# Moving four loads of a graph attention kernel to other places in the DMA queue

## Chip, cores and metric

The kernel runs on one core of a Trainium2 chip. The metric is the device time of one execution in microseconds, the median of several runs; lower is better. TensorE (PE in the profile) multiplies matrices and reads its weights with separate load instructions (PEld); VectorE is DVE, ScalarE is ACT, GpSimd is POOL. SyncE (SP) does no arithmetic here: its sequencer (SPq) issues the DMAs of the main loop one after the other, and a DMA that has to wait for a semaphore holds up everything behind it in that queue.

## What is computed

For each of 16 batch entries there are 512 nodes with 512 features, and each node attends to the first 20 nodes. Cut to what matters here:

```python
row_zero = v.sum(-1) == 0                                  # flags: which rows of x are zero
q_exp = where(row_zero, 0, q)
self_feat = concat([v, q_exp]) @ W_self.T + b_self
output = self_feat
for d in range(2):                                         # adj and its transpose
    A = adj (d == 0) or swapaxes(adj, 1, 2) (d == 1), first 20 columns     # 11 int32 labels each
    cond, vb = A.sum(-1), A @ w_bias + b_bias              # mask, and a bias from the labels
    aff = (self_feat @ Wq.T + bq) . (kv @ Wk.T + bk) / sqrt(dh)            # 16 heads, dh = 32
    w = softmax(where(cond > 0, aff, NEG) + vb)
    output += heads(w @ kv) @ Wout + bout
return v + relu(output)
```

## The kernel before

**Set-up** (lines 453 to 760) folds the key projections into the queries' weights and writes to DRAM what each batch entry needs later: the keys `g_d`, the values `bd_d` (fetched as `vd`), the score biases `cq_d`.

**The main loop** (lines 781 to 963) runs over the entries b, and in each over four tiles nt of 128 nodes. Everything is in float32. The order on each engine is written out by hand. Entry b+1 is prepared while entry b is worked on. TensorE's order within one entry, from the output product on, is:

- nt = 2: `attend(b-1)` (line 426, 48 small matmuls into the four banks `ps_o`: the weighted values of the entry before, called the output product here), the scores of tile 2 (line 353, 128 matmuls into `ps_s`), products 1 and 2 of entry b+1 (line 279). The self features are computed with seven half-size products in place of eight, numbered 1 to 7; 1, 4, 6 and 7 go to `ps_a`, 2 to `ps_d`, 3 and 5 to `ps_c`.
- nt = 3: product 6, the scores of tile 3, products 7 and 5.
- then entry b+1 begins. nt = 0: product 4, the scores of tile 0 in two parts (feature blocks 0 and 1 of the keys, then 2 and 3), and product 3, which is the last of the seven.
- nt = 1: the scores of tile 1.

VectorE takes the scores from `ps_s` (`weigh`, lines 367 to 375), ScalarE exponentiates (380), VectorE sums and inverts (406, 407), GpSimd scales (408), VectorE transposes (415). VectorE also adds the flag term to the products (`partial`, line 286, which needs the flags `nz`). GpSimd adds masks and biases of a tile (`full_add`, line 341, which needs `cq`) and x to the output (`residual`, line 444). ScalarE multiplies the labels of a half (two tiles) by the weights (`mask_mul`, line 314, which needs `adj`) and spreads the result over heads (334).

**SP's queue in one entry b** (for 0 < b < 15), with what each DMA waits for:

- nt = 0: x of b+1 in two halves (line 105), the first behind the exp of the tile before, the second behind `partial(b, 4)`; the flags of b+1 to DRAM (171, behind `row_mask` on GpSimd); the first half of the masks, `adj(b+1, 0)` (114), behind `mask_sum` of b.
- nt = 1: the flags read back to all partitions, `nz` (175), behind the exp of tile 0; the score biases `cq`, four DMAs (119); the second half of the masks, `adj(b+1, 1)`, behind `normal` on GpSimd.
- nt = 2: the rows of x of b+2 for the flags, `xn`, in two halves (109), the first behind the first of the four additions of `finish` (435), the second behind its first relu (439); the first half of the keys (130) behind the exp of tile 2.
- nt = 3: the output of b-1, blocks 0 and 1 (449, each behind its `residual`); the second half of the keys behind `mask_sum(b+1, 0)`; output block 2; the values `vd` (136); output block 3 follows at the next nt = 0.

`adj` has three buffers, `nz`, `cq` and `xn` have two. A manual dependency is added by `behind(dma, instruction)` (line 95).

Of the kernel before, what the change touches and what calls it, by code (L numbers as in the profile page):

```python
# [18 lines left out]
def gat_kernel(  # L19
# [81 lines left out]
    def load_x(b, ks=range(C), ins=None):  # L101
        if ks[0] == 0:
            xs[b] = load.tile([P, C, N], F32, tag="x", name=f"x{b}", bufs=3)
        at = slice(ks[0], ks[-1] + 1)
        behind(nc.sync.dma_start(xs[b][:, at], xT[b].rearrange("(c p) n -> p c n", p=P)[:, at]), ins)
# [5 lines left out]
    def load_adj(b, h, ins=None):  # L111
        t = adjs[b, h] = load.tile([P, 2, S * L], I32, tag="adj", name=f"adj{b}_{h}", bufs=3)
        a = adj[b, h * 2 * P : (h + 1) * 2 * P].rearrange("(t p) d m l -> p t (d m l)", p=P)
        behind(nc.sync.dma_start(t, a), ins)
# [317 lines left out]
    def finish(b, o, banks):  # L432

        for c in range(C):
            add = nc.vector.tensor_add(o[:, c], banks[c], sfs[b][:, c])  # L435
            if c == 0:
                done["add"] = add
        for c in range(C):
            relu = nc.scalar.activation(o[:, c], o[:, c], AF.Relu, bias=bo[:, c : c + 1])  # L439
            if c == 0:  # L440
                done["relu"] = relu

    def residual(b, c, o):
        nc.gpsimd.tensor_add(o[:, c], o[:, c], xs[b][:, c])  # L444
        outs.append((b, c, o))
# [323 lines left out]
    with tc.manual_schedule():  # L769
# [11 lines left out]
        for b in range(B):  # L781
            more = b + 1 < B
# [6 lines left out]
            for nt in range(NT):  # L789
# [22 lines left out]
                if nt == 0:  # L812
                    if b == 0:
                        for g in range(2):
                            scores(b, nt, g, ps[g])
                        mask_sum(b, 1)
                    else:
                        mask_mul(b, 1)
                        product(b, 4)
                        for g in range(2):  # L820
                            scores(b, nt, g, ps[g], range(2))
                        normal(*prev)
                        partial(b, 4, 1, 0, block(b, 1, 0))
                        if more:
                            load_x(b + 1, range(2), done["exp"])
                            load_x(b + 1, range(2, C), done["partial"])
                        for g in range(2):
                            scores(b, nt, g, ps[g], range(2, C))
                        if more:
                            row_mask(b + 1)  # L830
                        mask_count(b, 1)
                        joined(b, 3, "c", 1, 1)
                        product(b, 3)
                        mask_sum(b, 1)
                        if more:
                            load_adj(b + 1, 0, done["masks"])
                    mask_spread(b, 1, (0, 1))
                    if last:
                        biased = work.tile([P, C, N], F32, tag="o", name="biased")
                        for c in (2, 3):  # L840
                            nc.scalar.activation(biased[:, c], sfs[b][:, c], AF.Identity, bias=bo[:, c : c + 1])
                    s = weigh(b, nt, pair)
                    expo(s)
                    mask_spread(b, 1, (2, 3))
                    if prev is not None:
                        turn(*prev)
                    full_add(b, 1)
                    if more:
                        x_sum(b + 1, 1)
                    else:  # L850
                        for c in (2, 3):
                            nc.gpsimd.tensor_add(biased[:, c, N - P :], biased[:, c, N - P :], xs[b][:, c, N - P :])

                if nt == 1:
                    if b > 0:
                        joined(b, 2, "c", 0, 1)
                    if b > 0 and more:
                        load_nz(b + 1, done["exp"])
                        load_cq(b + 1)
                    normal(*prev)  # L860
                    if b > 0 and more:
                        load_adj(b + 1, 1, done["normal"])
                    if b == 0:
                        self_feat(0, 1, 1)
                    for g in range(2):
                        scores(b, nt, g, ps[g])
                    if b == 0:
                        self_copy(0, 1, 1)
                    if last:
                        for c in (0, 1):  # L870
                            nc.scalar.activation(biased[:, c], sfs[b][:, c], AF.Identity, bias=bo[:, c : c + 1])
                    s = weigh(b, nt, pair)
                    expo(s)
                    turn(*prev)
                    if more:
                        x_sum(b + 1, 2)
                        x_sum(b + 1, 3)
                    full_add(b, 2)
                    if last:
                        for c in (0, 1):  # L880
                            nc.gpsimd.tensor_add(biased[:, c], biased[:, c], xs[b][:, c])  # L881

                if nt == 2:
                    if more:
                        mask_mul(b + 1, 0)
                    else:
                        full_add(b, NT - 1)
                    if b > 0:
                        banks = [bank(f"ps_o{b - 1}_{q}", q) for q in range(4)]
                        attend(b - 1, banks)  # L890
                        o = work.tile([P, C, N], F32, tag="o", name=f"o{b - 1}")
                        finish(b - 1, o, banks)
                        if b + 2 < B:
                            load_xn(b + 2, 0, done["add"])
                            load_xn(b + 2, 1, done["relu"])
                    normal(*prev)
                    for g in range(2):
                        scores(b, nt, g, ps[g])
                    if more:
                        product(b + 1, 1)  # L900
                        product(b + 1, 2)
                    s = weigh(b, nt, pair, (lambda: partial(b + 1, 1, 0, 0)) if more else None)
                    expo(s)
                    turn(*prev)
                    if b > 0 and more:
                        load_keys(b + 1, range(2), done["exp"])
                    if more:
                        full_add(b, NT - 1)
                    if b > 0:
                        for c in (0, 1):  # L910
                            residual(b - 1, c, o)

                if nt == 3 and more:
                    mask_count(b + 1, 0)
# [131 lines left out]
```

## Time and profile before

| | us |
|---|---|
| runs of the kernel before | 590.48, 591.52, 591.87 (median 591.52) |
| the profiled execution, its own time | 593.27 |
| span of its profile, first to last instruction | 591.5 |
| mean granted TensorE clock | 0.995 |

How to read the views: the page gives each engine's busy time and its share of the span. The chain that ended last lists, in order of time, the work that each step waited for: start, duration, engine, tile, line, count; "issue" is time in which the engine waited for nothing that the profile shows. The view of waits gives, for an engine and a line, who ended its idle time, the total, the count and the longest. The timeline lists instructions in order of time (start, duration, engine, line, operation, tiles, count). The view of windows gives for a stretch its length, then each engine's busy time and number of instructions, the clock, the mean busy share of the 16 DMA engines and the GB/s. The DMA view lists queues (packets, MB, share of the DMA engines) and issues (count, size of each, median time from issue to landing).

### The profile page before, as it was taken

Reading aid. Unit: us, or ns where it says so; the run is one execution under the profiler, and the core shown is the slowest. Engines: PE = TensorE matmul, PEld = TensorE weight load, DVE = VectorE, ACT = ScalarE, POOL = GpSimd, SP = SyncE. Lnnn points to the kernel's source line nnn. Section 1 sums busy time; section 2 is a strip of 40 time slices with the busy share of each in tenths; the row PEclk is TensorE's granted clock in tenths of the full one; section 3 lists DMA queues with packets and bytes.
Section 4 is the critical chain, followed back from the end, with each engine's and each line's share of the span. In section 5 each row is a group of like instructions: output and inputs, shape, how many; then the busy total and the mean of one; then the engine's idle time right before and its main releaser. Section 6 shows DMA issues by size and latency. Waiting matters only on the chain.

```text
span 591.5 us, 30038 instructions
## 1 busy us (share of the span) xinstructions
PE 578.7 (98%) x13180; PEld 439.7 (74%) x13180; DVE 492.3 (83%) x785; ACT 395.6 (67%) x1162; POOL 384.2 (65%) x351
## 2 busy tenths in 40 slices
PE   8999999999999999999999999999999999999994
PEld 6654547888978687787878787788787878787882
DVE  0495565889898888999999999888989898989896
ACT  1234644587877677768686868677787877777661
POOL 2315663638677675758686777675858677776774
PEclk9999999999999999999999999999999999999997
DMA  8998999857848485767676766757585748582503
GB/s 294 385 406 299 332 376 329 257 126 199 223 154 229 155 236 148 206 168 209 184 208 163 223 173 202 171 181 208 164 217 170 216 149 232 158 238 85 167 13 142
DMA packets 98129, 124.10 MB, mean 210 GB/s; under 512 B 19952, under 2 KB 70160, under 8 KB 95952
## 3 DMA queue, kind: packets, MB, share of 16 engines
q1 hardware_dynamic: 96752, 120.31, 67.1%
q8 instruction: 103, 1.69, 1.2%
q0 software_dynamic: 672, 1.36, 1.0%
q10 hardware_dynamic: 576, 0.53, 0.3%
q14 instruction: 26, 0.21, 0.1%
HBM read 82.30 MB, written 40.24 MB: 207 GB/s over the span
## 4 chain that ended last, share of the span: by engine, by line
PE 94%; DVE 3%; DMA 1%; issue 1%; ACT 0%; POOL 0%; SPq 0%; DVEq 0%; POOLq 0%; ACTq 0%
PE ps_s L353 44%; PE ps_a L279 17%; PE ps_c L279 8%; PE ps_o L426 6%; PE ps_d L279 4%; PE ps_v L644 3%; PE ps_k L581 3%; PE ps_sf L202 2%; DMA ws_q<-in_wsT 1%; PE ps_kv L532 1%; DVE o L435 0%; PE ps_nz L186 0%; DVE wt L415 0%; DVE ps_s L371 0%; DVE sm L406 0%
## 5 line engine op out<-in xcount | busy, mean ns | idle before, releaser
L353 PEld LDWEIGHTS ps_s<-g,sf 128*32 128x32 f32 x8192 | 264.0, 110 | 19.8 <-issue 12.2
L353 PE MATMUL ps_s<-g,sf 128*32 128x152 f32 x8192 | 277.3, 293 | 0.5 <-ACT st L684 0.5
L334 ACT COPY both<-add 32x80 f32<-32x80 f32 x512 | 130.9, 256 | 54.8 <-DVE add L325 49.0
L408 POOL TENSOR_TENSOR s<-s,sm 128x640 f32<-128x640 f32 x63 | 80.3, 1275 | 98.0 <-DVE sm L407 98.0
L341 POOL TENSOR_TENSOR full<-cq,both 128x640 f32<-128x640 f32 x64 | 100.1, 1565 | 30.3 <-issue 24.3
L314 ACT ACTIVATE prod<-adj,wb_sb 128x80 f32<-128x80 int32 x330 | 112.5, 432 | 0.0
L380 ACT ACTIVATE s<-s 128x640 f32<-128x640 f32 x63 | 46.5, 738 | 69.4 <-DVE s L375 69.0
L444 POOL TENSOR_TENSOR o<-o,x 128x512 f32<-128x512 f32 x60 | 75.9, 1285 | 0.0
L367 DVE TENSOR_TENSOR full<-ps_s,full 128x608 f32<-128x608 f32 x63 | 49.1, 779 | 32.1 <-PE ps_s L353 26.6
L406 DVE TENSOR_REDUCE sm<-s 128x32 f32<-128x640 f32 x63 | 50.9, 808 | 8.8 <-ACT s L380 8.6
L279 PE MATMUL ps_a<-t,ws_s 128*32 128x246 f32 x960 | 55.5, 370 | 0.0
L371 DVE TENSOR_REDUCE ps_s<-full 128x32 f32<-128x640 f32 x63 | 52.2, 828 | 2.2
L415 DVE STREAM_TRANSPOSE wt<-s 128x640 f32<-128x640 f32 x63 | 52.8, 839 | 0.1
L375 DVE TENSOR_TENSOR s<-full,ps_s 128x640 f32<-128x640 f32 x63 | 51.6, 818 | 1.1
L426 PE MATMUL ps_o<-wt,vd 32*32 32x512 f32 (+5 forms) x816 | 40.8, 581 | 3.7 <-DVE wt L400 2.0
L279 PEld LDWEIGHTS ps_a<-t,ws_s 128*32 128x32 f32 x960 | 32.2, 110 | 15.5
L325 DVE TENSOR_REDUCE add<-prod 128x80 f32<-128x960 f32 x32 | 36.8, 1150 | 6.3 <-ACT prod L314 4.4
L244 POOL TENSOR_TENSOR t<-x 128x492 f32<-128x492 f32 x30 | 34.4, 1148 | 10.1 <-DVE full L367 5.2
L439 ACT ACTIVATE o<-o,bo 128x512 f32<-128x512 f32 x60 | 38.2, 708 | 0.6 <-POOL biased L881 0.6
L435 DVE TENSOR_TENSOR o<-ps_o,sf 128x512 f32<-128x512 f32 x60 | 36.8, 672 | 1.0 <-PE ps_o L426 1.0
L286 DVE SCALAR_TENSOR_TENSOR u<-nz,qw,ps_a 128x246 f32<-128x246 f32 x90 | 36.6, 449 | 0.0
L244 POOL TENSOR_TENSOR t<-x,t 128x492 f32<-128x492 f32 x30 | 34.4, 1147 | 1.2
(238 smaller groups left out, 722.7 us busy)
## 6 DMA issues: line engine op xcount, KB each, us to landing
g_d<-st SPq DMA_DIRECT2D x16, 1064.0 KB, 5.9
g<-g_d SPq DMA_DIRECT2D x28, 608.0 KB, 5.2
out_T<-o SPq DMA_DIRECT2D x60, 256.0 KB, 4.7
xn<-in_xn SPq DMA_DIRECT2D x28, 512.0 KB, 3.6
x<-in_xT SPq DMA_DIRECT2D x28, 512.0 KB, 4.3
adj<-in_adj SPq DMA_DIRECT2D x32, 440.0 KB, 5.0
nz<-nz_d SPq DMA_DIRECT2D x14, 256.0 KB, 4.0
wk<-in_wkT SPq DMA_DIRECT2D x2, 1024.0 KB, 8.0
```

Source lines behind the costliest of these rows:

```text
L244: nc.gpsimd.tensor_sub(t, one, two)
L279: nc.tensor.matmul(to, lhs, x[:, k], start=start, stop=stop, skip_group_check=n != 2)
L314: nc.scalar.activation(p[:, :, l], a[:, :, l], AF.Identity, scale=wb_sb[:, l : l + 1])
L334: nc.scalar.copy(adds[b, h][bass.ts(a, R), :, g], add[r].rearrange("p (t m) -> p t m", t=2))
L341: nc.gpsimd.tensor_add(f, cqs[b].unsqueeze(1).to_broadcast(shape), adds[b, nt // 2][:, nt % 2].unsqueeze(2).to_broadcast(shape),)
L353: nc.tensor.matmul(bank[bass.ts(a, R), bass.ts(j, WD // HL)], sfs[b][:, k, bass.ds(nt * P + (2 * g + j) * R, R)], keys[:, k, a], start=(k ...
L371: nc.vector.tensor_reduce(mx, f, AX.X, ALU.max)
L375: nc.vector.tensor_sub(s, f, mx.unsqueeze(3).to_broadcast(full))
L408: done["normal"] = nc.gpsimd.tensor_mul(s, s, sm.unsqueeze(3).to_broadcast(full))
L415: nc.vector.transpose(wts[b][:, nt], s.rearrange("p a h m -> p (a h m)"))
L426: nc.tensor.matmul(banks[a][bass.ds(at // 2 * DH, n * DH)].rearrange("p (t n) -> p t n", n=32), vd[r, bass.ds(at * DH, n * DH)], wt[r, :, ...
L444: nc.gpsimd.tensor_add(o[:, c], o[:, c], xs[b][:, c])
```

## The change

In every entry b from 1 to 14:

- `adj(b+1, 0)` is issued directly behind the second half of x, ahead of the flags' write to DRAM, with no wait of its own (it waited for `mask_sum` before).
- `nz` is issued in nt = 2, after `finish` in program order, with the same kind of wait (the last exp, now that of tile 1).
- `done["add"]` becomes the last of the four additions in `finish`, so the first `xn` waits for the fourth addition in place of the first.
- after the residuals of blocks 0 and 1 in nt = 2 the output of these blocks is stored there (before: at the start of nt = 3, the next place in SP's queue), and behind the stores come `adj(b+1, 1)` and the four DMAs of `cq`, with no wait of their own.

Nothing else is touched: the same loads, of the same sizes, and the same arithmetic.

```diff
@@ finish
             add = nc.vector.tensor_add(o[:, c], banks[c], sfs[b][:, c])
-            if c == 0:
-                done["add"] = add
+            done["add"] = add
@@ nt == 0
                             load_x(b + 1, range(2), done["exp"])
                             load_x(b + 1, range(2, C), done["partial"])
+                            load_adj(b + 1, 0)
...
                         mask_sum(b, 1)
-                        if more:
-                            load_adj(b + 1, 0, done["masks"])
@@ nt == 1
                         joined(b, 2, "c", 0, 1)
-                    if b > 0 and more:
-                        load_nz(b + 1, done["exp"])
-                        load_cq(b + 1)
                     normal(*prev)
-                    if b > 0 and more:
-                        load_adj(b + 1, 1, done["normal"])
@@ nt == 2
                         finish(b - 1, o, banks)
+                        if more:
+                            load_nz(b + 1, done["exp"])
                         if b + 2 < B:
                             load_xn(b + 2, 0, done["add"])
...
                             residual(b - 1, c, o)
+                        store()
+                        if more:
+                            load_adj(b + 1, 1)
+                            load_cq(b + 1)
```

## The prediction

> **What bounds the kernel now.** First the page.
>
> ```profile
> span 591.5 us, 30038 instructions
> ...
> PE 578.7 (98%) x13180; PEld 439.7 (74%) x13180; DVE 492.3 (83%) x785; ACT 395.6 (67%) x1162; POOL 384.2 (65%) x351
> ```
>
> TensorE is busy for 98% of the span. The change removes no work, so it can only win back time in which TensorE stands still. The second view, the chain in order of time, shows where that is. These are output products (line 426, the start of nt = 2) from three stretches of it.
>
> ```profile
> 164.12 2.60 PE ps_o L426 x47
> ...
> 195.02 1.04 PE ps_o L426 x25
> 196.06 0.39 issue
> 196.45 2.10 PE ps_o L426 x23
> ...
> 226.92 0.98 PE ps_o L426 x4
> ...
> 258.97 2.17 PE ps_o L426 x48
> ...
> 289.44 2.17 PE ps_o L426 x48
> ...
> 381.08 1.05 PE ps_o L426 x27
> ...
> 413.08 2.84 PE ps_o L426 x48
> ...
> 444.22 2.17 PE ps_o L426 x48
> ...
> 535.83 2.17 PE ps_o L426 x48
> ```
>
> An undisturbed entry takes 289.44 - 258.97 = 30.47 us. Five entries take longer: from 164.12 to 195.02 it is 30.90, then 31.90, then 32.05 (to 258.97); from 381.08 32.00, then 31.14 (to 444.22). Over 30.48 that is 0.42 + 1.42 + 1.57 + 1.52 + 0.66 = **5.6 us**. The twelve entries from 164.12 to 535.83 take 371.71 against 12 x 30.48 = 365.76, so 5.95 us are lost in all, nearly all of it in these products. The loss is "issue": no semaphore ended it, and it begins behind 25, 4 or 27 matmuls, so no operand was missing at the start.
>
> What is left is the supply of instructions. The page's queue list has one for them, and the DMA view of two stretches (0 to 225.9, 0 to 288.55) and the windows say how far it had come.
>
> ```profile
> q8 instruction: 103, 1.69, 1.2%
> ...
> q8 instruction: 31, 0.51, 0.9%
> ...
> q8 instruction: 44, 0.72, 1.0%
> ```
>
> ```profile
> 0.00:225.90 225.90, 221.91 (x4117) 159.77 (x4121) 165.71 (x276) 130.37 (x373) 125.22 (x128) 1.00 0.82 264
> 0.00:288.55 288.55, 284.09 (x5688) 208.45 (x5692) 221.61 (x362) 177.29 (x514) 169.20 (x166) 1.00 0.79 247
> ```
>
> 1.69 MB in 103 packets are 16.4 KB each, and TensorE's 2 x 13180 instructions over 103 are 256 a packet: q8 feeds TensorE. Ahead of the stalled product at 226.92, 31 packets had started for 4117 + 4121 = 8238 instructions, 302 more than 31 x 256. Ahead of the clean one at 289.44, 44 packets for 11380, 116 more. So in the stalled entry the next packet came 186 instructions later than in the clean one, and TensorE ran dry. Why late? Part of SP's queue in a clean entry, from the timeline (output product at 289.44), and sizes from the DMA view:
>
> ```profile
> 293.45 4.10 SPq L109 DMA_DIRECT2D xn<-in_xn  x2
> ...
> 300.18 0.38 SPq L130 DMA_DIRECT2D g<-g_d  x1
> 300.97 1.17 SPq L449 DMA_DIRECT2D out_T<-o  x2
> 304.48 0.38 SPq L130 DMA_DIRECT2D g<-g_d  x1
> ...
> 309.54 2.30 SPq L105 DMA_DIRECT2D x<-in_xT  x2
> 312.40 0.34 SPq L171 DMA_DIRECT2D nz_d<-nz  x1
> 314.45 0.37 SPq L114 DMA_DIRECT2D adj<-in_adj  x1
> 317.69 0.34 SPq L175 DMA_DIRECT2D nz<-nz_d  x1
> 318.08 2.49 SPq L119 DMA_DIRECT2D cq<-cq_d  x3
> ```
>
> ```profile
> g<-g_d SPq DMA_DIRECT2D x28, 608.0 KB, 5.2
> ...
> adj<-in_adj SPq DMA_DIRECT2D x32, 440.0 KB, 5.0
> nz<-nz_d SPq DMA_DIRECT2D x14, 256.0 KB, 4.0
> ...
> cq<-cq_d SPq DMA_DIRECT2D x64, 20.0 KB, 3.6
> ```
>
> From 314.45 to the product at 319.92, masks, flags and biases are in flight, 440 + 256 + 80 KB. **My theory**: an instruction packet waits behind the transfers issued before it, and one that falls due there comes when the store is empty. An entry of 784 matmuls is 6.1 packets, so the packets' places drift from entry to entry; that is why the stalls come in two groups and other entries are clean.
>
> [...]
>
> **The change, part by part.** Taken away from the stretch ahead of the output product: `adj(b+1, 0)`, `nz`, `cq`, and `adj(b+1, 1)` beside it. The masks move up behind x, and nothing is then issued until nt = 2. I count the 5.6 us as gone: **-5.6**.
>
> Added, first: 440 KB directly behind x. A packet waiting behind x now waits behind the masks as well. Two stretches give the rates, one with keys and output and the fastest microsecond I found.
>
> ```profile
> 300.30:305.40 5.10, 5.10 (x152) 4.75 (x148) 4.44 (x8) 3.35 (x12) 4.93 (x6) 1.00 0.80 222
> ...
> 396.00:397.00 1.00, 1.00 (x40) 1.00 (x36) 1.00 (x2) 0.00 (x0) 1.00 (x1) 1.00 1.13 383
> ```
>
> 440 KB take 1.1 us at 383 GB/s and 2.0 us at 222. A packet falls due every 30.48 / 6.1 = 5.0 us; the stretch in which it can be caught, from the second x (309.54 + 2.30 - 0.39 = 311.45) to where the masks stood (314.45), is 3 us minus what comes too late to matter, say 2.5: half a packet an entry, 7 in 14 entries. Room: scores use 256 instructions in 4.13 us, 62 a us, so the 186 instructions between clean and stalled are 3 us. Bounds are 0 (all fit) and 7 x 2.0 = 14 us. I take the low side, 0.3 us each, because the clean entry from 258.97 to 289.44 holds two loads of keys of 608 KB and loses nothing: **+2.1**.
>
> [...]
>
> Second: `adj(b+1, 1)` and `cq`, 520 KB, stand between the output's stores and the second keys (304.48). Packets that wait behind these keys wait 1.4 to 2.3 us longer. The stretch is some 1.7 us, a third of a packet an entry, 5 in all; bounds 0 and 5 x 2.3 = 11.5; by the same row as before 0.3 us each: **+1.5**.
>
> Third, the second keys themselves. SP issues the masks (0.37) and four `cq` (three take 2.49) behind the second store, which ends at 300.97 + 1.17 = 302.14: at 2.49 / 3 = 0.83 each, 302.14 + 0.37 + 3.3 = 305.8; at the 0.34 that the flags' issue takes, 303.9, ahead of the wait that ends at 304.48. So the keys leave 0 to 1.3 us later, and 520 KB are ahead of them. They landed at 304.48 + 5.2 = 309.7. Their first use is the second part of the scores of tile 0:
>
> ```profile
> 309.99 4.13 PE ps_s L353 x128
> ...
> 292.19 0.74 ACT L380 ACTIVATE s<-s 128x640 f32<-128x640 f32 x1 [2.85 <-DVE s L375]
> ...
> 292.77 2.45 DVE L435 TENSOR_TENSOR o<-ps_o,sf 128x512 f32<-128x512 f32 x4
> ...
> 297.74 0.85 DVE L286 SCALAR_TENSOR_TENSOR u<-nz,qw,ps_a 128x246 f32<-128x246 f32 x2
> ...
> 300.21 0.63 ACT L166 ACTIVATE xn<-xn 128x512 f32<-128x512 f32 x1
> ...
> 308.88 1.57 POOL L341 TENSOR_TENSOR full<-cq,both 128x640 f32<-128x640 f32 x1 [1.52 <-issue]
> ...
> 314.34 0.78 DVE L367 TENSOR_TENSOR full<-ps_s,full 128x608 f32<-128x608 f32 x1
> ```
>
> That part starts at 309.99 + 4.13 / 2 = 312.05: room 2.35 us. I take the middle, 0.6, and the quick rate for the 520 KB, 1.4, as part of them passes while SP is still issuing: 2.0 late, hidden, **0**, by a narrow margin. Bounds: 0 and, with 1.3 + 2.3 = 3.6 late, 1.25 us an entry, 17.5 in 14.
>
> The other waits. `nz` is released by the exp (292.19 + 0.74 = 292.93) and lands 4.0 later, at 296.9; `partial` wants it at 297.74, room 0.8, beside fewer loads than before. Queued behind it on SP is only `xn`. That now waits for the fourth addition, 292.77 + 2.45 = 295.22, in place of 293.45: 1.8 us later. By `nz`'s 4.0 it lands at 299.2, ahead of its reader at 300.21; the second half still waits for the relu. `cq` leaves by 305.8 and lands by 309.4, with the load ahead up to 311.7; `full_add` on GpSimd wanted it at 308.88 and its result is wanted at 314.34, so 3.9 us cover that, with what GpSimd has queued behind it. The masks' second half, issued by 302.5, is read behind the same exp that releases x at 309.54, 7 us for a landing of 5.0; the first half is read in nt = 2, later still. If one of these covers were gone, it would cost what it is late in each of 14 entries. All **0**.
>
> Sum: -5.6 + 2.1 + 1.5 = **-2.0 us**. The profiled execution took 593.27 of its own time (span 591.5 and 1.77 around it), 1.75 above the median of 591.52; against it the sum gives 591.3, and against the median **589.5**.
>
> **Rivals.** (A) *All of it is won.* [...] For it: the seven other entries of the twelve lose 0.35 us together, under loads of 608 KB. [...] 13%.
>
> (B) *Nothing moves.* The stalls follow the loads to their new places and cost the same, or the store empties in the output product for a reason of its own. 591.5. For it: the loss sits in that product alone, though loads are in flight everywhere. Against it: the seven entries with a clean product have the same matmuls in it. [...] 17%.
>
> (C) *Slower by the keys.* If the second keys land over 2.35 us later, TensorE waits in the scores of tile 0 of each of 14 entries. Price: at 2.7 us late, 0.35 x 14 = 4.9 us; 589.5 + 4.9 = 594.4; at the bound 607. It decides from 2.35 us. For it: the DMA engines are 0.80 busy in the stretch from 300.3 already. Against it: the room. 17%.
>
> (D) *Slower by displaced packets.* x, masks and flags in one run catch seven packets with all of the 1.5 us, the keys five with 0.5: 591.52 - 5.6 + 10.5 + 2.5 = 598.9; halfway to the forecast's price 594. 11%.
>
> **How the numbers follow.** Forecast 42%, with its own range 586.9 (added terms of 1.0) to 590.3 (of 4.4). 0.2%, 1.2 us, is about what a measurement of this kernel can tell from no change. Faster: 0.42 + 0.13 = 0.55; same: 0.17; slower: 0.17 + 0.11 = 0.28. The range reaches from A, 585.5, over B to the middle of C and D, 597.0; beyond it lie the far ends of C and D, about 15%.
>
> **What would show it.** Right: output products of 2.17 us throughout and entries of 30.48 except a few; the second keys landing before the scores' second part; `nz` never a releaser. First added term: pieces of scores or product 3 longer than 4.13 and 1.66, with "issue", some 5 us behind x. Second: the same around products 7, 5 and 4. C: "PE ps_s <- DMA g" in the waits, in each entry. Wrong altogether: the same five products stall with no load in flight (B).

## The result and the profile after

The changed kernel takes **597.45 us** (median of six runs, 594.24 to 599.71), the kernel before 591.3 (six runs, 590.36 to 592.32): 1.0102 times as long, 95% interval 1.0066 to 1.0138. The forecast was 589.5 with a range up to 597.0. The sign was wrong, and the time lies just outside the range.

The profiled execution took 594.24, the quickest of the six, so its rows show the loss at its smallest. Two more executions were profiled for that reason (599.22 and 596.82; below after_2 and after_3). First the page after:

```profile
span 592.5 us, 30013 instructions
PE 577.5 (97%) x13180; PEld 439.0 (74%) x13180; DVE 491.1 (83%) x785; ACT 396.3 (67%) x1162; POOL 384.6 (65%) x351
...
g<-g_d SPq DMA_DIRECT2D x28, 608.0 KB, 5.5
...
adj<-in_adj SPq DMA_DIRECT2D x32, 440.0 KB, 6.3
nz<-nz_d SPq DMA_DIRECT2D x14, 256.0 KB, 3.2
```

The work is the same; TensorE is busy a little shorter and stands still longer. The masks take 6.3 us to land (5.0 before), the flags 3.2 (4.0 before). The chain in order of time, the same output products as in the prediction and the pieces of scores ahead of some:

```profile
194.27 2.17 PE ps_o L426 x48
...
286.36 2.17 PE ps_o L426 x48
...
312.70 2.32 PE ps_s L353 x70
315.02 0.18 issue
315.20 2.23 PE ps_s L353 x58
317.43 2.17 PE ps_o L426 x48
...
379.66 2.67 PE ps_o L426 x48
...
467.63 3.09 PE ps_s L353 x93
470.72 1.04 issue
471.76 1.48 PE ps_s L353 x35
473.24 2.17 PE ps_o L426 x48
...
521.02 5.68 DMA g<-g_d
...
526.84 2.35 PE ps_s L353 x62
```

The products that stalled before are 2.17 us long now, all but one. What stalls instead is the last block ahead of them, the scores of tile 1: 1.04 us at 470.72, behind 93 of its 128 matmuls. (The piece of 5.68 us at 521.02 is not a loss of 5.68 us: the chain names what came last, and by the blocks before it the second part of the scores could have begun at 526.74, 0.1 us earlier.) The view of waits says the same in sums; the first fence is before, the second after:

```profile
PEld ps_o L426 <- issue: 21.9, 37, 1.5
...
PEld ps_s L353 <- issue: 12.2, 15, 0.8
```

```profile
POOL full L341 <- DMA cq<-cq_d: 21.9, 10, 3.2
...
PEld ps_s L353 <- issue: 17.6, 25, 1.3
PEld ps_o L426 <- issue: 17.4, 33, 0.8
POOL t L244 <- DMA x<-in_xT: 12.9, 11, 4.2
```

Before TensorE's weight loads, "issue" takes 4.5 us less in the output product (line 426) and 5.4 us more in the scores (line 353). GpSimd has two new waits, for the score biases (ten times) and for x (eleven times). SP's queue in one entry (output product at 286.36) shows what was moved where:

```profile
299.06 0.47 SPq L114 DMA_DIRECT2D adj<-in_adj  x1
299.58 2.13 SPq L119 DMA_DIRECT2D cq<-cq_d  x4
302.35 0.60 SPq L130 DMA_DIRECT2D g<-g_d  x1
...
307.04 1.86 SPq L105 DMA_DIRECT2D x<-in_xT  x2
308.94 0.46 SPq L114 DMA_DIRECT2D adj<-in_adj  x1
309.50 0.42 SPq L171 DMA_DIRECT2D nz_d<-nz  x1
```

The second keys leave 302.35 - 286.36 = 15.99 us behind the start of the output product (before 304.48 - 289.44 = 15.04), x 20.68 (20.10), the first masks 22.58 (25.01), straight behind x.

**The same packet before and after.** Where the scores of tile 1 stall, one instruction packet can be followed through both kernels: the 81st of q8. Up to these two moments 80 had started, and 81 had 0.1 or 0.15 us later. First the kernel before (output product at 444.22), then after_2 (at 445.17), each in turn the window, the count of packets, SP's rows, and for after_2 the chain:

```profile
0.00:469.75 469.75, 464.75 (x10272) 350.29 (x10276) 385.16 (x614) 314.80 (x928) 300.49 (x280) 1.00 0.74 226
```

```profile
q8 instruction: 80, 1.31, 1.1%
```

```profile
464.31 2.30 SPq L105 DMA_DIRECT2D x<-in_xT  x2
...
469.23 0.37 SPq L114 DMA_DIRECT2D adj<-in_adj  x1
```

```profile
0.00:474.20 474.20, 466.19 (x10375) 351.96 (x10378) 386.86 (x619) 318.22 (x938) 302.01 (x280) 1.00 0.70 225
```

```profile
q8 instruction: 80, 1.31, 1.1%
```

```profile
466.37 1.84 SPq L105 DMA_DIRECT2D x<-in_xT  x2
468.26 0.46 SPq L114 DMA_DIRECT2D adj<-in_adj  x1
```

```profile
471.51 3.09 PE ps_s L353 x93
474.60 1.85 issue
```

Before, the packet started 469.75 - 444.22 = 25.5 us behind the output product, 68 instructions (10272 + 10276 - 80 x 256) past the last one's end. In after_2 it started at 29.0 us, 273 instructions past, 0.4 us before TensorE ran dry for 1.85 us. Before, x stood ahead of it and the masks had left only 0.5 us earlier; after, x was 1.1 us later and the masks had left 5.9 us earlier, straight behind it.

**What ends a pause.** The trace also keeps the start of every q8 packet, of every matmul and of every weight load. In the 14 entries of all 20 profiles of this study there are 59 stretches of over 0.6 us in which TensorE starts neither a matmul nor a weight load. 55 of them end 2.2 to 2.5 us behind the start of a q8 packet, among them all 20 of the changed kernel's three profiles and all 6 of the two of the kernel before. Packets are some 5 us apart (6.1 in an entry of 30.5 us), so by chance about one stretch in sixteen would end there. By these 55 of 59, a missing instruction packet is what TensorE waits for, before and after the change; which transfer had held the packet up is not in these records.

**Where the time is lost**, for all kernels of this study. For each block of the entry (its length from the start of its first matmul to the start of the next block) the excess over the clean length is summed over 14 entries. The blocks are those of each run's chain; for e11 and e12 they are TensorE's own rows, as in the first of the 14 entries the chain of e11 runs over VectorE. Clean are 2.17 us for the output product, 4.27 for the scores of tile 2, 4.13 for the others, 1.66 for a product. All excess counts every block, the shorter ones too, and so is not quite the sum of the four columns:

```
us lost in             output    products  scores   scores   all      span
14 entries             product   7 and 5   tile 0   tile 1   excess
before                 5.55      0.02      0.08     0.47     6.06     591.5
before_2               4.48      0.02      0.08     0.73     5.23     589.4
after                  0.50      1.90      1.30     5.09     8.61     592.5
after_2                0.60      0.51      2.52     9.75     13.21    597.4
after_3                0.32      1.03      1.97     7.09     10.35    595.0
e1_masks0              0.21      0.42      0.07     2.16     3.07     588.1
e2_rest                3.38      0.23      1.67     3.60     8.83     594.3
e3_early               0.51      0.00      0.71     5.48     6.64     590.5
e4_spread              0.08      0.93      0.19     0.72     1.75     587.4
e5_early_nt1           0.00      0.00      0.54     0.73     1.21     587.0
e6_dummy               0.72      0.29      0.14     2.47     3.49     587.8
e7_masks_back          2.36      0.51      0.03     0.20     3.25     588.2
e8_flags_back          0.00      0.57      0.38     0.78     1.69     586.0
e9_late_keys           0.91      1.04      1.75     1.83     5.25     590.6
e10_before_noflags     0.23      0.55      0.14     0.55     1.36     585.3
e11_after_noflags      0.00      0.83      1.97     6.68     9.75     592.7
e12_after_flags_first  1.47      0.92      1.47     5.57     10.77    595.1
e13_e4_flags_first     1.15      0.00      0.07     2.30     4.55     590.0
e14_late_x             0.00      1.13      0.59     0.67     2.32     588.6
e15_late_x_noflags     0.00      0.36      0.00     0.71     1.08     587.8
```

The spans differ also by what the set-up took, so the columns show the place and the medians below the size.

### The profile page after: what moved, and what is told of

It is laid out like the page before. It is cut to its first block, busy times and chain, and to the rows that moved or that the text cites. A ratio compares the mean times of both kernels' runs of the same rounds, so it can differ in the third digit from the quotient of the medians.

```text
span 592.5 us, 30013 instructions
## 1 busy us (share of the span) xinstructions
PE 577.5 (97%) x13180; PEld 439.0 (74%) x13180; DVE 491.1 (83%) x785; ACT 396.3 (67%) x1162; POOL 384.6 (65%) x351
## 3 DMA queue, kind: packets, MB, share of 16 engines
q8 instruction: 103, 1.69, 1.1%
## 4 chain that ended last, share of the span: by engine, by line
PE 93%; DVE 3%; issue 1%; DMA 1%; ACT 0%; POOL 0%; DVEq 0%; POOLq 0%; ACTq 0%
PE ps_s L353 44%; PE ps_a L279 16%; PE ps_c L279 8%; PE ps_o L426 5%; PE ps_d L279 4%; PE ps_v L643 3%; PE ps_k L580 3%; PE ps_sf L202 2%; PE ps_kv L531 2%; DMA g<-g_d 1%; PE ps_warm L490 1%; DVE o L435 0%; DVE full L367 0%; DVE ps_s L371 0%; PE ps_nz L186 0%
## 5 line engine op out<-in xcount | busy, mean ns | idle before, releaser
L353 PE MATMUL ps_s<-g,sf 128*32 128x152 f32 x8192 | 280.3, 293 | 3.5 <-issue 2.8
L341 POOL TENSOR_TENSOR full<-cq,both 128x640 f32<-128x640 f32 x64 | 100.2, 1566 | 38.4 <-DMA cq<-cq_d 21.9
L426 PE MATMUL ps_o<-wt,vd 32*32 32x512 f32 (+5 forms) x816 | 36.9, 579 | 2.3 <-DVE wt L400 2.0
L166 ACT ACTIVATE xn<-xn 128x512 f32<-128x512 f32 x56 | 34.7, 620 | 2.8 <-DMA xn<-in_xn 2.7
```

Of the source, the lines that this page charges most:

```text
L341: nc.gpsimd.tensor_add(f, cqs[b].unsqueeze(1).to_broadcast(shape), adds[b, nt // 2][:, nt % 2].unsqueeze(2).to_broadcast(shape),)
L353: nc.tensor.matmul(bank[bass.ts(a, R), bass.ts(j, WD // HL)], sfs[b][:, k, bass.ds(nt * P + (2 * g + j) * R, R)], keys[:, k, a], start=(k ...
L426: nc.tensor.matmul(banks[a][bass.ds(at // 2 * DH, n * DH)].rearrange("p (t n) -> p t n", n=32), vd[r, bass.ds(at * DH, n * DH)], wt[r, :, ...
```

## The experiments

The theories named in the expectations are these. **I**: an instruction packet waits behind the loads issued before it, and TensorE runs dry; the change has only moved the place. **K**: the second keys, issued later, come too late for the scores of tile 0. **G**: GpSimd, which now waits for the biases and for x, holds up the chain from scores to exponentials. Later ones are named where they come.

### One part of the change at a time

e1 adds to the kernel before only the move of the first masks:

```diff
                             load_x(b + 1, range(2, C), done["partial"])
+                            load_adj(b + 1, 0)
...
                         mask_sum(b, 1)
-                        if more:
-                            load_adj(b + 1, 0, done["masks"])
```

> The kernel before with one part of the change: the first half of the masks is issued straight behind x; everything else stays. Theory K (the second half of the keys comes late, because masks and score biases stand ahead of it in the queue and on the DMA engines): nothing stands ahead of the keys here, so no worse than before, 589 to 592. Theory I (TensorE's instruction packets wait behind loads; x and masks in one run catch them): stalls with issue as the releaser appear in the scores of tile 1, as in the changed kernel (there some 4 us in the profiled run), and the output products lose some of theirs, since masks are gone from ahead of them but flags and biases are not: 590 to 595. Theory G (GpSimd waits for score biases and x, and everything behind it is late): 589 to 592.

Measured: 589.82 (ten runs), ratio 0.9990, interval 0.9966 to 1.0013: no difference. The products lose 0.21 in place of some 5, the scores of tile 1 gain 2.16. By itself the move wins a little in the profile, and little enough that the runs can't tell it from nothing. The time is K's and G's, a little under I's range; the stalls in the scores of tile 1 are I's sign.

e2 is the changed kernel with this move taken back:

```diff
-                            load_adj(b + 1, 0)
...
                         mask_sum(b, 1)
+                        if more:
+                            load_adj(b + 1, 0, done["masks"])
```

> The changed kernel without that part: the first half of the masks goes back behind mask_sum; flags, second masks and score biases are in their new places. Theory K: the second keys are as late as in the changed kernel, landing 21 to 22.7 us after the output product begins, against a use at 22.6; so 594 to 599, about the time of the changed kernel. Theory I: no packet is caught behind x and masks, the output products stall less than before as only one load is left ahead of them: 588 to 591. Theory G: the biases are as late as in the changed kernel: 594 to 599.

Measured: 596.21 (four runs), 1.0093 (1.0061 to 1.0125): nearly all of the harm lies in the other part, the loads that moved to nt = 2. The time is in the range of K and of G and some 5 us over I's, which looked for harm behind x alone. But in the views of waits of e2 and of the changed kernel no wait of TensorE in the main loop ends with a DMA or with GpSimd. With no masks straight behind x, the scores of tile 1 lose 3.60 us and those of tile 0 1.67. The product stalls are in part back as well, here three of the four in the chain:

```profile
194.84 2.88 PE ps_o L426 x48
...
226.02 3.26 PE ps_o L426 x48
...
381.36 3.10 PE ps_o L426 x48
```

e3 is the changed kernel with the second masks and the biases issued ahead of the two output stores:

```diff
                     if b > 0:
+                        if more:
+                            load_adj(b + 1, 1)
+                            load_cq(b + 1)
                         for c in (0, 1):
                             residual(b - 1, c, o)
                         store()
-                        if more:
-                            load_adj(b + 1, 1)
-                            load_cq(b + 1)
```

> The changed kernel with the second masks and score biases issued ahead of the output's two stores, not behind them, so that SP is through with them when the second keys become due. The same bytes stand ahead of the keys. Theory K, by issue time: the second keys leave at 15.1 us after the output product's start as before, land by 21, and most of the loss goes: 589 to 593. Theory K, by bytes: the keys still land at 21.5 to 22.7 and the time stays at 594 to 599. Theory I alone: 593 to 599, as the packets wait as long as in the changed kernel. Theory G: the biases come 2 us earlier: 589 to 593.

Measured: 592.01 (ten runs), 1.0022 (0.9998 to 1.0046). The same bytes, 1.6 us earlier in the same slot (medians), cost 5.4 us less by the medians. The second keys leave at 15.7 us behind the start of the output product (median over the entries but the first; 16.4 in the changed kernel, 15.1 before), the first half of x at 20.2 (21.0; 20.2). The wait for the biases on GpSimd, 21.9 us in the changed kernel, is gone from its view of waits, yet the scores of tile 1 lose 5.48 in its profile: that wait is not what they wait for. The time is again K's (by issue time) and G's, and under I's.

### The changed kernel and the one before once more

These are single executions, for their profiles.

> The changed kernel again, for a second profile, since its first profiled run was the quickest of its six. Theory K (second keys late): a run near 597 has more entries in which the scores of tile 0 stand 22 to 23 us behind the start of the output product, 4 us in all or more. Theory I (instruction packets): the loss is in the scores of tile 1, 27 to 30 us behind, 7 us or more, and the keys' part stays near 1 us.

> The changed kernel a third time, with the same expectations as the second: K, 4 us or more at the scores of tile 0; I, 7 us or more at the scores of tile 1.

> The kernel before again, for a second profile, since its first was above its median. Both theories: the loss is in the output product, in the same two groups of entries (packets drift by the same count in every run), 3 to 5 us; nothing at the scores of tile 0.

Measured: 599.22, 596.82 and 591.14. The scores of tile 1 lose 9.75 and 7.09 us against 0.73, and the output products 0.60 and 0.32 against 4.48. In every profile of the changed kernel most of the loss sits in the scores, those of tile 1 above all.

### The loads spread over the entry

e4 leaves the slot to the output's stores and puts the first masks into nt = 1, the second masks back to their old place, and the biases behind them. Against the changed kernel:

```diff
-                            load_adj(b + 1, 0)
...  nt == 1
+                    if b > 0 and more:
+                        load_adj(b + 1, 0, done["exp"])
                     normal(*prev)
+                    if b > 0 and more:
+                        load_adj(b + 1, 1, done["normal"])
+                        load_cq(b + 1)
...  nt == 2
                         store()
-                        if more:
-                            load_adj(b + 1, 1)
-                            load_cq(b + 1)
```

> The same loads spread out: first masks in nt = 1 behind the exp of tile 0, second masks at their old place behind the scaling, score biases directly behind them, flags in nt = 2 as in the changed kernel. Nothing stands ahead of the second keys, nothing directly behind x, and one load is in flight at a time around the output product. Theory K: no worse than before, 589 to 592, as the keys are where they were. Theory I: the output products keep a stall or none, and no packet is caught elsewhere: 585.5 to 588. Theory G: 589 to 592, as the biases come later than before but ahead of their use.

Measured: **587.78** (nine runs, 586.74 to 589.14), **0.9943 (0.9927 to 0.9958)**: quicker than both kernels, in I's range and below that of K and G. Of SP's rows of one entry, and the output product that follows:

```profile
427.85 2.38 SPq L105 DMA_DIRECT2D x<-in_xT  x2
430.71 0.34 SPq L171 DMA_DIRECT2D nz_d<-nz  x1
436.00 3.38 SPq L114 DMA_DIRECT2D adj<-in_adj  x2
```

```profile
438.23 2.17 PE ps_o L426 x48
```

880 KB of masks leave right ahead of and beside the output product, and it loses nothing (0.08 us in 14 entries). So loads as such beside this product are not what stalled it before.

e5 is e3 with the first masks in nt = 1 (the line `load_adj(b + 1, 0, done["exp"])` ahead of `normal`, as in e4, in place of the one behind x):

> The kernel of the third experiment (second masks and biases ahead of the output's stores) with the first masks taken away from behind x and issued in nt = 1 behind the exp of tile 0. Theory I: the 5.9 us that the third experiment lost in the scores of tile 1 go, since nothing is behind x any more: 585.5 to 588. Theory K: the first masks do not touch the second keys, so the time stays at 590 to 593.

Measured: 589.04 (ten runs), 0.9961 (0.9940 to 0.9981). Against e3 only the masks are no longer behind x, and 5.48 us of loss in the scores of tile 1 become 0.73. The time lies between I's range and K's.

### One load, one place: e4 with a single edit

Four kernels change e4 at one point each. The differences to e4 are those of the ratios to the kernel before, times 591.3 us, since not all ran on one chip.

e6 adds a load of 440 KB behind x into a tile that nobody reads, and changes nothing else:

```diff
                             load_x(b + 1, range(2, C), done["partial"])
+                            spare = xsum.tile([P, 2, S * L], I32, tag="spare", name=f"spare{b}")
+                            behind(nc.sync.dma_start(spare, adj[b + 1, : 2 * P].rearrange(...)), None)
```

> The spread kernel with one extra load that nothing reads: 440 KB of masks straight behind the second half of x, into a spare tile. Theory I (packets wait behind whatever is in flight): stalls come back in the scores of tile 1, by what the kernel with only the masks moved showed there, 1.7 us, or more, as the masks themselves follow in nt = 1 here: 589 to 592. Theory K and theory G: nobody waits for this load and no key, bias or x stands behind it at once, so no change: 587 to 588.5.

Measured: 591.83 (ten runs), 1.0011 (0.9992 to 1.0030): (1.0011 - 0.9943) x 591.3 = 4.0 us more than e4, interval 2.6 to 5.5. It is in I's range. No engine waits for that tile, so K and G can't make this. Its profiled run is the quickest of the ten (that of e4 the slowest of its nine) and shows 1.7 us of them, 3.49 against 1.75; from its chain:

```profile
193.77 2.49 PE ps_o L426 x45
...
284.74 0.46 issue
...
468.80 0.32 issue
```

e7 puts the first masks back to where they stood before the change (`load_adj(b + 1, 0, done["masks"])` behind `mask_sum(b, 1)`):

> The spread kernel with the first masks put back to where the kernel before had them, behind mask_sum, 3.3 us earlier than in the spread kernel; flags and biases stay away from the output product. Theory I: the packets that fall due 24.5 to 25.6 us behind the start of an entry wait behind the masks again, but nothing follows them, so the output products lose a part of what they lost before: 588.5 to 590.5. Rival: the flags and biases alone made the stalls of the kernel before: 587 to 588.5.

Measured: 591.5 (ten runs), 0.9997 (0.9981 to 1.0014), 3.2 us more than e4 and 1 us over I's range. The masks leave at 219.56, 2.1 us behind the flags' write, and the product behind them stalls:

```profile
217.52 0.34 SPq L171 DMA_DIRECT2D nz_d<-nz  x1
219.56 6.65 SPq L114 DMA_DIRECT2D adj<-in_adj  x2
```

```profile
225.19 2.97 PE ps_o L426 x48
```

e8 puts flags and biases back to nt = 1 instead, straight behind the first masks (`load_nz(b + 1, done["exp"])` and `load_cq(b + 1)` there, and gone from their places in e4):

> The spread kernel with flags and biases put back into nt = 1, straight behind the first masks (which stay in nt = 1): 776 KB in one run from 28.3 us on, close ahead of the output product. Theory I: packets due 27 to 30 us behind the start of an entry wait for the whole run, but they have the output product and the scores behind it before them; 588 to 591, with stalls in the scores of tile 2, not in the output product. Rival (loads ahead of the product as such make the stalls): the output products stall as in the kernel before: 590 to 592.

Measured: 588.94 (four runs), 0.9952 (0.9937 to 0.9967), 0.5 us more than e4 and within the uncertainty of it. From SP's rows and from the chain:

```profile
405.56 0.37 SPq L114 DMA_DIRECT2D adj<-in_adj  x1
406.03 0.41 SPq L175 DMA_DIRECT2D nz<-nz_d  x1
```

```profile
407.82 2.17 PE ps_o L426 x48
```

Masks, flags, biases and masks in a row, 440 + 256 + 80 + 440 KB, leave from 2.3 us ahead of an output product that loses nothing. The time is in I's range, but the stalls that I expected in the scores of tile 2 are missing. Of the four loads that the change takes away from the product, only the first masks, at +25 us behind the flags' write, stall it by themselves (e7): by 2.36 us, about half of the 4.48 to 5.55 before. What made up the other half is not settled.

e9 issues the second keys behind the third output store, 17.2 us behind the start of the output product in place of 15.1:

```diff
                     mask_sum(b + 1, 0)
-                    if b > 0:
-                        load_keys(b + 1, range(2, C), done["masks"])
...
                         residual(b - 1, 2, o)
                         store()
+                        load_keys(b + 1, range(2, C), done["masks"])
                         load_values(b)
```

> The spread kernel with the second half of the keys issued behind the third store of the output, some 2 us later than before and as late as in the latest entries of the changed kernel, with nothing else moved. Theory K: if lateness of the keys were the larger part of the loss, some entries stand at the scores of tile 0 and the time rises by 3 us or more: 591 to 595. Theory I: the keys land at about 22.3, just ahead of their use at 22.6; at most 0.3 us in some entries: 587.5 to 590.

Measured: 591.18 (ten runs), 1.0002 (0.9982 to 1.0023), 3.5 us more than e4. That is in K's range, not in I's. But K's sign is missing: the keys landed by 22.23 us in every entry, ahead of their use at 22.6, no wait of TensorE on them stands in its view of waits, and its stalls (5.25 us) are spread over the products and both scores. What this run does show is that moving the keys toward x costs about as much as the 440 KB of e6 (3.5 us against 4.0), without a byte added.

### The write of the flags

Where masks stall the product, the small write of the flags stands 2 us ahead of them. Theory **W**: that write holds the DMA engines. Theory **V**: the bytes of x and masks alone do. e10 is the kernel before, e11 the changed kernel, both without that write from entry 3 on:

```diff
-        behind(nc.sync.dma_start(nzs[b], nz_d[b : b + 1].partition_broadcast(P)), ins)
+        behind(nc.sync.dma_start(nzs[b], nz_d[2:3].partition_broadcast(P)), ins)
...
-                        if more:
+                        if b == 1:
                             row_mask(b + 1)
```

> Left out: the flags of entries 3 to 15 are neither computed on GpSimd nor written; every entry reads the flags of entry 2, with the same load of 256 KB. All other loads stand where they stand before the change. Theory W: the small write of the flags (2 KB, 5 us to landing; in the stretch behind it the DMA engines are 0.66 busy and move only 50 GB/s) holds the engines, and the packets that come late in the output product wait for it together with the masks behind it. Then 4 to 5.5 us go: 586 to 587.5, and the output products are 2.17 us. Theory V: the packets wait for the bytes of x and of the masks alone; then the output products go on losing 4 us or more and the time stays at 590.5 to 591.5.

Measured: 587.98 (six runs), 0.9954 (0.9937 to 0.9971): 2.7 us less than before, interval 1.7 to 3.7. W expected 4 to 5.5, V none: the size lies between them, and the sign is W's, as the output products lose 0.23 us in place of some 5. The windows from 25.88 to 28.28 us behind the start of a product, first before, then e10, show the masks pass:

```profile
190.00:192.40 2.40, 2.40 (x75) 2.09 (x68) 2.33 (x4) 1.98 (x7) 0.67 (x1) 1.00 0.66 50
```

```profile
219.50:221.90 2.40, 2.40 (x80) 2.26 (x72) 2.37 (x4) 1.99 (x7) 0.34 (x1) 1.00 0.60 198
```

With the write ahead, the engines are 0.66 busy and move 50 GB/s; without it they are 0.60 busy and move 198. Over 13 entries this stretch moves 183 to 206 GB/s in e10. Before it moves 35 to 65 in ten of them, and 152 to 190 in the three that begin with a product that stalled by over 1 us. (e10 also takes the flags' computation off GpSimd; that this has no part in it was not tried by itself.)

> Left out: the same flags, in the changed kernel: x and the first masks follow each other with nothing behind them until the second half. Theory W: the write behind the masks is a good part of what the packets wait for; most of the 5 to 10 us in the scores of tile 1 go: 589 to 592. Theory V: 1,464 KB of keys' rest, x and masks in one run are the cause, and 2 KB more or less change nothing: 596 to 598.5.

Measured: 595.21 (four runs), 1.0090 (1.0057 to 1.0124). That is just under V's range and 3 us over W's. The scores of tile 1 lose 6.68 us in its profile, between the quickest run of the changed kernel and the third. After the change the write is not the main cause.

e12 and e13 leave nothing out and write the flags before x leaves, in the changed kernel and in e4:

```diff
...  nt == 0
-                        if more:
-                            row_mask(b + 1)
...  nt == 3
                         residual(b - 1, 3, o)
+                    if b + 2 < B:
+                        row_mask(b + 2)
                     full_add(b + 1, 0)
```

> Nothing is left out: in the changed kernel the flags are computed and written ahead of the last score bias addition of nt = 3, so that their write stands ahead of x in the queue and no longer behind the masks. Theory W: the write is out of the stretch with x and masks, 590 to 593, unless it delays x in its place. Theory V: no change, 596 to 598.5.

Measured: 599.01 (four runs), 1.0133 (1.0095 to 1.0170), a little over V's range.

> The best version so far (first and second masks and biases in nt = 1, flags read in nt = 2) with the flags written ahead of x. It lost 1.75 us in all in its profile, with the write behind x and nothing behind it. Theory W: some of these 1.75 us go, 586 to 587.5. Theory V: no change, 587 to 588.5. If the write ahead of x delays x, 588 to 590.

Measured: 591.85 (twelve runs), 1.0012 (0.9994 to 1.0030), 4.1 us more than e4: worse than any of the three ranges named. x leaves 0.9 us later (21.1 in place of 20.2), so theory **L** was formed: a late x is what costs.

e14 tries L alone, on e4:

```diff
-                            load_x(b + 1, range(2), done["exp"])
+                            load_x(b + 1, range(2), done["partial"])
```

> The best version (masks and biases in nt = 1) with the first half of x released by the same addition as the second half, so that it leaves 1.9 us later (22.1 in place of 20.2 us behind the start of the output product); nothing else changes, no load is added. Theory L: what is dear in the changed kernel is that the second keys and x leave about a microsecond late, so that keys, x and what stands behind them pass in one run while packets fall due; then 590 to 593 with stalls in the scores of tile 1. If only the added bytes count (440 KB of masks behind x), nothing changes: 587 to 588.5.

Measured: 588.52 (twelve runs), 0.9942 (0.9922 to 0.9962): no difference to e4. L falls: in e4's order the first half of x may leave 1.9 us later at no cost.

> The same late x, and left out: the flags of entries 3 to 15 are neither computed nor written; every entry reads those of entry 2. If the write behind a late x is what holds the packets (the theory that held before the change, where its removal gave 3.3 us), the time falls back to 586.5 to 588. If the late x alone holds them, it stays within 1 us of the version with the write: 589.5 to 593.

Measured: 588.33 (twelve runs), 0.9948 (0.9924 to 0.9973): the write is no cost in e4's order either.

## Why the prediction was wrong

**The stalls that go: right.** The forecast took 5.6 us away from the output products; three profiles of the changed kernel lose 0.32 to 0.60 us there, those of the kernel before 5.55 and 4.48. The reason was half right. Of the loads named, flags and biases beside the product do no harm by themselves (e8, 0.00 us lost there), nor do two masks in a row (e4, 0.08); the first masks at +25 us do (e7, 2.36), and with them in place nearly all of the stall goes when the flags' write ahead of them goes (e10, 0.23 left), a neighbour that the prediction did not weigh.

**The two added terms, at 0.3 us a packet: the step that failed.** The prediction bounded them by 0 and 14 us (masks behind x) and 0 and 11.5 us (loads ahead of the second keys), and took the low side, +2.1 and +1.5, because one clean entry held keys of 608 KB. Outside the output products the three profiles of the changed kernel lose 8.1, 12.6 and 10.0 us against 0.5 and 0.75 before: 7.4 to 12.1 us more, not 3.6. Single stalls were 1.04 and 1.85 us, not 0.3. The clean entry was the wrong neighbour: keys with a gap behind them are not x with masks straight behind (the scores of tile 1 lose 5.48 us with these masks in e3, 0.73 without in e5).

The first term is some 4 us and not 2.1: 4.0 us for a load that nobody reads (e6 against e4), and for the masks themselves 0.9961 - 1.0022 = -0.0061, 3.6 us (e5 against e3). The second was missed by more, and in its place too. The prediction looked for it around products 7, 5 and 4. e2, with no masks straight behind x, loses 3.60 us in the scores of tile 1 and 1.67 in those of tile 0; outside the output products it loses 5.45 us in all, 4.7 to 4.9 more than before, against the +1.5.

**The slot's effect on keys and x was not seen.** SP, with five DMAs more to issue in the slot, sends the second keys 1.3 us later and the first half of x 0.8 us later (medians). The same loads ahead of the stores (e3) cost 5.4 us less; with the masks taken away from x too (e5), the scores of tile 1 lose 0.73. By the ratios the two edits about add up: the move of the first masks alone costs nothing net (e1, 0.9990), as it wins in the output product and loses in the scores; the rest costs 5.5 us (e2, 1.0093); both are 1.0102.

**Keys late, 0 by a narrow margin: right in size.** In the chain after they come last once, 0.1 us late. All that the scores of tile 0 lose is 1.3 to 2.5 us, issue stalls included, against a bound of 17.5. Keys that leave late do cost (3.5 us in e9), but not by this wait.

**The covers.** Flags, rows of x and second masks cost TensorE nothing that its waits show. `cq` came when forecast: the last of its four DMAs landed 19.9 us behind the start of the output product (median), forecast 20.0 to 22.3. GpSimd waits for it ten times, up to 3.2 us, within the 3.9 that the prediction found behind `full_add`. With that wait gone (e3) the scores of tile 1 go on losing.

**Rivals.** A (all won) and B (nothing moves) are out. The price that the prediction takes for A, 585.5, the low end of its range, needs the masks straight behind x to cost nothing; no run shows that, and a load of their size in that place, read by no engine, cost 4.0 us (e6). C, keys that TensorE waits for, is not the cause. D, displaced packets, fits best what was measured (55 of 59 pauses end 2.2 to 2.5 us behind a packet's start, e6 costs 4.0 us); its halfway price, 594, is the quickest run, its full price of 598.9 is 1.45 over the median. It had been given 11%. That its sum comes so near is in part luck: it put 10.5 us on x, masks and flags and 2.5 on the keys, while e2 loses most of it with no masks behind x and leaving out the flags' write (e11) wins nothing clear.

A store of ready instructions, which the prediction's theory and B speak of, stands in no view of these runs. Measured is that in after_2 TensorE ran dry some 0.4 us after the 81st packet had started, and that 5 to 13 us of some 590 to 597 are lost before and after, in the profiles of the two kernels.

**What stays open.** The records tie TensorE's stalls to instruction packets (55 of 59 pauses), and the runs show three things that cost time here: a load straight behind x (e6 4.0 us, e3 against e5 3.6), second keys issued later (e9 3.5) and masks straight behind the flags' write (e7 3.2; 2.7 won in e10). Argued, and not shown, is that the slot of the output does its harm through the later keys and x. Why e13 costs 4.1 us (its write stands ahead of x, but a late x alone costs nothing) and why e9 costs 3.5 us with the keys in time is not settled: the profiles show stalls scattered over the blocks, not the transfer that each packet waited for. What a packet itself waits for was not tried.

## What to carry to other kernels

TensorE, 97 to 98% busy in this kernel, had one more input, its own instructions, which came through the DMA engines (q8, 103 packets, 1.69 MB): "issue" in the chain that begins in the middle of a block was the sign, and 55 of 59 pauses ended 2.2 to 2.5 us behind a packet's start. Look for the same in another kernel. Before a load is moved, write down what stands ahead of it and behind it in the queue, and when the last of that run lands; a free place for the issue was not a free place for the bytes (4.0 us in e6). Here the same bytes with gaps between them (e4) are 0.57% quicker than before (interval 0.42 to 0.73) and, by the medians, 1.6% quicker than the changed kernel (587.78 to 597.45).

## What the hardware showed beside that

The DMA view's row for the write of the flags, first before, then after:

```profile
nz_d<-nz SPq DMA_DIRECT2D x14, 2.0 KB, 4.5
```

```profile
nz_d<-nz SPq DMA_DIRECT2D x14, 2.0 KB, 6.1
```

A write of 2 KB took 4.5 us to land before the change and 6.1 after it. In the 2.4 us shown above the DMA engines were 0.66 busy at 50 GB/s with it, 0.60 at 198 GB/s without it: the busy share did not tell how many bytes moved. And a load that nobody waits for was not free: 440 KB an entry, read by no engine, cost 4.0 us in 14 entries (e6), 0.3 us each.
